# Moving projection tails, maxima transposes and head variances within the attention steps of a four-layer sequence model

## The chip, the cores and the metric

One core of a Trainium2 chip runs the whole program in one launch. The metric is device time in microseconds (us). Everything is fp32.

## The reference

The input is four sequences (batches) of 512 tokens with 288 features. A rotation comes first, then three transformer layers, numbered 0, 1 and 2 here, each with adaptive layer norms, 16-head attention of head size 18, and a feed-forward part; in layer 2 that is a mixture of four experts. The change touches attention alone. In layer 1 every head's q and k are normalised before they are used:

```python
qkv = (xn @ w_qkv + b_qkv).reshape(B, N, 3, H, hd)
q, k, v = (qkv[:, :, 0], qkv[:, :, 1], qkv[:, :, 2])
q = _ln(q, 1e-05, qn_g, qn_b)
k = _ln(k, 1e-05, kn_g, kn_b)
attn = jnp.einsum('bqhd,bkhd->bhqk', q, k) * scale
attn = jax.nn.softmax(attn, axis=-1)
o = jnp.einsum('bhqk,bkhd->bqhd', attn, v).reshape(B, N, C)
```

Layers 0 and 2 compute the same without the two `_ln` lines.

## The kernel before

Layer and batch make one number n = 4·layer + batch, from 0 to 11. `attend` (L1207) runs n's attention in 32 **steps**: four groups of four heads, and eight steps s = 0 to 7 in each. The order of the work on TensorE, VectorE and ScalarE is written out by hand: instructions stay in the order in which the Python code issues them. Only transfers and GpSimd's work are placed by a scheduler.

A step issues the following.

- **Scores for maxima**, `maxima` (L1119): two matmuls into the PSUM tile `p_s`, queries by keys, and on VectorE one reduction of the tile to row maxima, into `M`. They run LOOK = 10 steps ahead, so from step 22 on they belong to the next n.
- **Scores for weights**, `weigh` (L1137): two matmuls into `p_st`, keys by queries, and one exponential on ScalarE. The four score matmuls contract over 32 rows each, so they sit in the four 32-row strips of the array and run side by side. `p_s` and `p_st` share one pool of two PSUM buffers (L82).
- **Transposed maxima**, `take_maxima` (L1129), once in a group at s = 6: four transposes of `M` into `p_m`, and a VectorE subtraction from the queries. The first use of those queries is two steps later.
- **Values**, `give_values` (L1237), in even steps: four matmuls into `p_av`; after a group's last, ScalarE copies the sum to `o`, and five transfers store it.
- **Filling work** (`fill`): generators that are advanced until a budget `left` is spent. It grows in each step by total/32, half a microsecond more in odd steps and half a microsecond less in even ones (L1223). A generator yields the cost of what it issued.

The fill holds above all `project(n+1)` (L1044), which makes the next n's q, k and v. It has five q/k slices (`qk_job`, PSUM tile `p_qk`, 126 rows of output each, the last 72) and four v slices (`v_job`, `p_v`), taken in pairs. Of the 288 features, 256 are contracted in two **dense** matmuls for each slice (128 rows each). The last 32 are its **tail**: one matmul on 32 rows, and the two tails of a pair use different strips. Then each slice is evicted, in layer 1 in two halves:

```python
scalar.activation(sq, p[0:w], AF.Square, bias=bias)
vector.tensor_scalar(t, p[0:w], bias, None, ALU.add)
yield 0.0
matmul(pv[0:w], varsel..., sq, start=True, stop=True)
scalar.activation(rs, pv[0:w], AF.Ln, bias=eps5[0:w])
scalar.activation(rs, rs, AF.Exp, scale=-0.5)
yield 0.86
vector.scalar_tensor_tensor(t, t, gains[0]..., rs, ...)
nc.gpsimd.tensor_scalar(t, t, gains[1]..., None, ALU.add)
```

The second half (the variance matmul `p_var` and what follows) is kept in `later` and issued behind the next pair's dense matmuls. Each slice ends in a transfer from its `stage` tile (three buffers) to a scratch tensor `qd` in HBM (L1076). When all five are on their way, eight transfers read `qd` back in the padded layout of the scores: four for Q, four for K, one for each strip (L1113). K's four need the fifth slice, Q's only the first three. `there` then tells `attend` that the next n may be used.

Behind the projection's first part come `finish` (L1180, the output projection `p_o` of n−1, four pieces), the remaining v slices, and the layer norm transposes `p_t` for n−1's feed-forward part. What is left when the 32 steps end is issued then, and `mlp(n−1)` follows.

Projection tiles, `p_m`, `p_o`, `p_t` and `p_var` share one pool of three PSUM buffers (`pmm`, L79).

Of the kernel before, what the change touches and what calls it, by code (L numbers as in the profile page):

```python
# [9 lines left out]
F32 = mybir.dt.float32  # L10
# [6 lines left out]
B, T, C = 4, 512, 288  # L17
# [4 lines left out]
H, HD, HS = 16, 18, 32  # L22
VS = HD + 1
NG = 4
HP = 7
QP = HP * HD
QK = 2 * C
NQ = -(-QK // QP)
# [19 lines left out]
def cond_seq_kernel(ctx: ExitStack, tc: tile.TileContext, a: dict, out: bass.AP):  # L48
# [18 lines left out]
    dma = nc.sync.dma_start  # L67
# [159 lines left out]
    Q = [t[:, 0:NG * T].rearrange("p (g t) -> p g t", t=T) for t in store]  # L227
    K = [t[:, NG * T:2 * NG * T].rearrange("p (g t) -> p g t", t=T) for t in store]
# [7 lines left out]
    zero_row = rows.tile([4, NG * T], F32, name="zero_row")  # L236
# [398 lines left out]
    NB, LOOK = 3 * B, 10  # L635
# [33 lines left out]
    def layernorm(l, part, b, dst, norm):  # L669

        for _ in norm:
            pass
        for _ in to_featT(dst, b, XN.pop((l, part, b)), modT[l][:, 2 * part + 1], modT[l][:, 2 * part], 2 + part):
            yield 0.6
# [353 lines left out]
    with tc.tile_pool(name="attn", bufs=2) as at:  # L1028
# [14 lines left out]

        def project(n, norm):  # L1044

            l, b = divmod(n, B)
            wqk, wv = WA[l][:2]
            h = hT[0]
            yield from layernorm(l, 0, b, h, norm)
            qd = scratch.tile([2 * H, HD, T], F32, tag="qd", name=f"qd{n}")  # L1050
            flat = qd.rearrange("h d t -> (h d) t")

            def qk_job(m):
                w = min(QP, QK - m * QP)
                cols = slice(m * QP, m * QP + w)
                p = pmm(f"p_qk{n}_{m}")

                def evict():
                    bias = QB[l][0:w, m:m + 1]
                    t = at.tile([QP, T], F32, tag="stage", name=f"stage{n}_{m}", bufs=3)[0:w]  # L1060
                    if l != 1:
                        scalar.activation(t, p[0:w], AF.Identity, bias=bias, scale=scol[0:w, m:m + 1])
                    else:
                        tmp = at.tile([128, 2, T], F32, tag="e", name=f"tmp{n}_{m}", bufs=6)
                        sq, rs = tmp[0:w, 0, :], tmp[0:w, 1, :]
# [3 lines that stand above are left out]
                        pv = pmm(f"p_var{n}_{m}")  # L1069
                        matmul(pv[0:w], varsel.rearrange("p h d -> p (h d)")[0:w, 0:w], sq, start=True, stop=True)  # L1070
# [3 lines that stand above are left out]
                        vector.scalar_tensor_tensor(t, t, gains[0][0:w, m:m + 1], rs, ALU.mult, ALU.mult)  # L1074
                        nc.gpsimd.tensor_scalar(t, t, gains[1][0:w, m:m + 1], None, ALU.add)
                    dma(flat[cols], t)  # L1076
                return p[0:w], 0.86, lambda k, r: (wqk[r, k, cols], h[r, k, :]), evict

            def v_job(j):
                p = pmm(f"p_v{n}_{j}")  # L1080

                def evict():
                    (scalar.copy if j % 2 else vector.tensor_copy)(
                        V[n % 2][:, j, :, 0:HD], p[:, :C].rearrange("p (h d) -> p h d", d=HD))
                    yield from ()
                return p[:, :C], 0.49, lambda k, r: (h[r, k, j * 128:(j + 1) * 128], wv[r, k, :]), evict

            jobs = [(qk_job, m) for m in range(NQ)] + [(v_job, j) for j in range(NT)]
            later = []
            for i in range(0, len(jobs), 2):  # L1090
                pair = []
                for job, arg in jobs[i:i + 2]:
                    p, cost, operands, evict = job(arg)
                    for k in range(KW):
                        matmul(p, *operands(k, slice(0, 128)), start=(k == 0), stop=False)
                        yield cost
                    pair.append((p, operands, evict))
                for e in later:
                    yield from e
                for q, (p, operands, evict) in enumerate(pair):  # L1100
                    matmul(p, *operands(KW, strip(q)), start=False, stop=True)

                later = [e for e in [evict() for p, operands, evict in pair] if next(e, None) is not None]
                yield 0.95
                if i <= NQ - 1 < i + 2:
                    for e in later:
                        yield from e
                    later = []

                    src = qd.rearrange("(s g i) d t -> s i d g t", s=2, i=4)  # L1110
                    for s, t in enumerate((Q[n % 2], K[n % 2])):
                        for q in range(4):
                            dma(t[q * HS:q * HS + HD], src[s, q])  # L1113
                    for q in range(4):
                        dma(Q[n % 2][q * HS + HD:q * HS + VS], zero_row[q:q + 1].rearrange("a (g t) -> a g t", t=T))
                    there.add(n)
                    yield None

        def maxima(G, step):  # L1119
# [9 lines left out]
        def take_maxima(G):  # L1129

            n, g = divmod(G, NG)
            p = pmm(f"p_m{G}")
            for j in range(NT):
                transpose(p[:, j * 128:(j + 1) * 128], M[G % 2][:, j].rearrange("p h r -> p (h r)"), ident)
            vector.tensor_sub(Q[n % 2][:, g, :], Q[n % 2][:, g, :], p)
# [70 lines left out]

        def attend(n, fill, total, norms):  # L1207

            left = 0.0
            for step in range(8 * NG):  # L1210
                g, s = divmod(step, 8)
                G = NG * n + g
                ahead, mstep = divmod(8 * G + s + LOOK, 8)
                if ahead < NG * NB:
                    while ahead // NG not in there:
                        next(fill)
                    maxima(ahead, mstep)
                E.append(weigh(G, s))
                if s == 8 - 2 and G + 1 < NG * NB:
                    take_maxima(G + 1)  # L1220
                if s % 2 == 0:
                    give_values()
                left += total / (8 * NG) + (0.5 if s % 2 else -0.5)  # L1223
                next(norms, None)
                while left > 0:
                    cost = next(fill, "end")
                    if cost == "end":
                        break
                    left -= cost or 0.0
                if s % 2:  # L1230
                    ready.append((G, s // 2))
            for _ in fill:
                pass
            for _ in norms:
                pass

        def give_values():  # L1237

            if not ready:
                return  # L1240
            G, c = ready.pop()
            if c == 0:
                PO[0] = pacc(f"p_av{G}")
            sum_values(G, PO[0], c, E[:2])
            del E[:2]
            if c == NT - 1:
                t = at.tile([128, T], F32, tag="o", name=f"o{G}", bufs=3)
                scalar.copy(t, PO[0])
                n, g = divmod(G, NG)
                if g == 0:  # L1250
                    S[n] = (scratch.tile([H, T], F32, tag="sd", name=f"sd{n}"),
                            scratch.tile([H, HD, T], F32, tag="od", name=f"od{n}"))
                dma(S[n][0][4 * g:4 * g + 4, :], t.rearrange("(h r) c -> h r c", r=HS)[:, HD])
                for h in range(4):
                    dma(S[n][1][4 * g + h], t[h * HS:h * HS + HD])
# [29 lines left out]
        E, ready, PO, S, there, norms = [], [], [None], {}, set(), {}  # L1285
# [22 lines left out]
        new = project(1, norm1)  # L1308
        for _ in range(4):
            next(new)  # L1310
        for t in range(LOOK):
            maxima(*divmod(t, 8))
            if t == 8:
                take_maxima(0)
            next(rest, None)
            next(new)
            if t == 5:
                projection_bias(0)
        for n in range(NB):
            l, b = divmod(n, B)  # L1320
            last = n and divmod(n - 1, B)

            fill, side, total = [], [], 0.0
# [6 lines left out]
            if n + 1 < NB:  # L1330
                if n:
                    new = project(n + 1, norm)
# [26 lines left out]
            if n == NB - 1:  # L1359
                fill = [routed(norms[1], 1), place(0), fill[0]]  # L1360
# [196 lines left out]
```

## Time and profile before

| | us |
|---|---|
| median of three runs | 2061.03 |
| lowest and highest | 2056.3, 2065.32 |
| the profiled execution | 2073.42 |
| its span | 2071.7 |

The profiled execution is 12.4 us above the median. The mean granted TensorE clock over its span is 0.954. The page gives TensorE 1887.7 us of busy time (91% of the span), VectorE 928.4, ScalarE 783.6, GpSimd 251.9. The attention steps lie between about 188 and 1655 us.

In the timeline a step begins where the first weight load of its `p_s` stands. From the first of step 0 to that of step 31, an n takes:

| n | layer of n / of the projection in it | from, us | 31 steps, us |
|---|---|---|---|
| 2 | 0 / 0 | 431.05 | 86.9 |
| 3 | 0 / 1 | 563.50 | 92.5 |
| 4 | 1 / 1 | 695.92 | 92.8 |
| 5 | 1 / 1 | 828.71 | 103.3 |
| 6 | 1 / 1 | 971.94 | 92.5 |
| 7 | 1 / 2 | 1106.31 | 86.8 |
| 8 | 2 / 2 | 1233.02 | 86.7 |

A timeline row gives start, duration, engine, line, operation, output<-inputs, shapes, how many instructions were merged, and in brackets the engine's idle time before it with what ended it. Most rows carry L60, the line of the helper that keeps the order. PEld is a weight load, PE a matmul; each fp32 matmul stands as two of each. "issue" means that no wait shows.

### The profile page before, as it was taken

How to read it: one execution, taken by the hardware profiler on the slowest of the kernel's cores; microseconds unless marked ns; L12 is line 12 of the kernel's file. 1: busy time of each engine (PE TensorE's matmuls, PEld its weight loads, DVE VectorE, ACT ScalarE, POOL GpSimd, SP SyncE). 2: the span in 40 equal slices, each digit the busy share in tenths (PEclk: the TensorE clock that was granted, in tenths of full speed). 3: DMA queues.
4: the chain of work that ended last, by engine and by line, in shares of the span. 5: the costliest groups of instructions: out<-in, count | busy, mean ns of one | idle time of the engine just before them, and what ended most of it. 6: DMA issues, size and time to landing. Idle time of an engine off the chain costs nothing. (4 is left out here: it accounts for less than half of the span.)

```text
span 2071.7 us, 26248 instructions
## 1 busy us (share of the span) xinstructions
PE 1887.7 (91%) x10269; PEld 935.6 (45%) x10269; DVE 928.4 (45%) x1953; ACT 783.6 (38%) x1169; POOL 251.9 (12%) x362
## 2 busy tenths in 40 slices
PE   6769879999999999899999999998987888999998
PEld 4544223343523434234234353333332266788886
DVE  6764646346164362552644626345576234211111
ACT  5122454444254343453544434434444222221221
POOL 1000010001010020010100000000000122233232
PEclk9578999999999999999999999999999689999999
DMA  3212152031131221511213112161212265576673
GB/s 97 71 40 62 36 147 84 22 89 36 25 85 30 70 62 42 136 42 54 72 26 77 42 54 81 21 134 35 83 46 66 86 222 167 182 242 200 211 241 97
DMA packets 89419, 187.23 MB, mean 90 GB/s; under 512 B 25453, under 2 KB 50456, under 8 KB 86802
## 3 DMA queue, kind: packets, MB, share of 16 engines
q1 hardware_dynamic: 77462, 103.39, 19.1%
q0 software_dynamic: 11248, 79.79, 11.9%
q10 hardware_dynamic: 584, 2.36, 0.3%
q8 instruction: 81, 1.33, 0.3%
q14 instruction: 44, 0.36, 0.1%
HBM read 152.49 MB, written 55.45 MB: 100 GB/s over the span
## 5 line engine op out<-in xcount | busy, mean ns | idle before, releaser
L60 ACT ACTIVATE e<-p_st 128x1024 f32<-128x1024 f32 x384 | 392.7, 1023 | 650.7 <-PE p_st L60 646.3
L60 DVE TENSOR_REDUCE store<-p_s 128x2 f32<-128x1024 f32 x384 | 470.3, 1225 | 364.5 <-PE p_st L60 320.7
L60 PE MATMUL p_s<-store 32*128 32x512 f32 x1536 | 442.2, 648 | 82.5 <-DVE store L60 81.3
L60 PE MATMUL p_st<-store 32*128 32x512 f32 x1536 | 445.7, 659 | 0.9 <-DVE store L60 0.9
L60 PEld LDWEIGHTS p_s<-store 32*128 32x128 f32 x1536 | 120.0, 185 | 315.3 <-DVE store L60 228.2
L60 PE MATMUL p_av<-e,store 128*32 128x512 f32 x1536 | 212.8, 627 | 2.2 <-ACT e L60 2.2
L60 PE MATMUL p_he<-hTe,store 128*128 128x256 f32 (+1 forms) x1026 | 188.4, 390 | 4.2 <-DVE hTe L60 4.2
L60 PE MATMUL p_ye<-store,hide 128*128 128x288 f32 x684 | 171.4, 409 | 0.0
L60 PEld LDWEIGHTS p_he<-hTe,store 128*128 128x128 f32 (+1 forms) x1026 | 151.4, 191 | 37.7 <-issue 13.6
L695 POOL TENSOR_TENSOR x<-x,gated 128x288 f32<-128x288 f32 x80 | 63.9, 799 | 841.6 <-DVE gated L60 841.6
L60 PE MATMUL p_qk<-hT,wqk 128*126 128x512 f32 (+1 forms) x360 | 163.1, 622 | 0.3 <-DVE store L60 0.3
L60 ACT ACTIVATE hide<-p_he,store 128x256 f32<-128x256 f32 x171 | 68.5, 478 | 245.1 <-PE p_he L60 244.3
L60 PE MATMUL p_h<-hT,w 128*128 128x512 f32 (+1 forms) x432 | 153.5, 610 | 5.2 <-DVE store L60 5.2
L60 PEld LDWEIGHTS p_ye<-store,hide 128*128 128x128 f32 x684 | 128.2, 190 | 36.7 <-ACT hide L60 2.3
L60 PE MATMUL p_y<-w,hid 128*128 128x288 f32 x576 | 141.8, 407 | 0.0
L60 DVE TENSOR_TENSOR gated<-p_y,gate 128x288 f32<-128x288 f32 x32 | 14.6, 457 | 283.0 <-PE p_y L60 283.0
L60 PEld LDWEIGHTS p_y<-w,hid 128*128 128x128 f32 x576 | 108.8, 190 | 35.5 <-issue 6.1
L60 PEld LDWEIGHTS p_st<-store 32*128 32x128 f32 x1536 | 118.2, 187 | 12.1 <-issue 9.1
L60 PEld LDWEIGHTS p_h<-hT,w 128*128 128x128 f32 (+1 forms) x432 | 62.1, 189 | 95.1 <-issue 84.9
L60 PE MATMUL p_o<-wp,oc 126*128 126x288 f32 (+1 forms) x288 | 99.4, 468 | 1.3 <-DVE oc L60 1.3
L60 PEld LDWEIGHTS p_qk<-hT,wqk 128*126 128x126 f32 (+1 forms) x360 | 47.1, 178 | 95.9 <-issue 94.3
L60 DVE COPY hTe<-p_te 128x512 f32<-128x512 f32 x19 | 13.1, 690 | 169.2 <-PE p_tf L60 117.8
(248 smaller groups left out, 1728.8 us busy)
## 6 DMA issues: line engine op xcount, KB each, us to landing
store<-qd SPq DMA_DIRECT2D x96, 144.0 KB
qd<-stage SPq DMA_DIRECT2D x48, 252.0 KB
od<-o SPq DMA_DIRECT2D x192, 36.0 KB
rd<-rd SPq DMA_DIRECT2D x12, 576.0 KB
oc<-od SPq DMA_DIRECT2D x24, 252.0 KB
rb<-rd SPq DMA_DIRECT2D x24, 252.0 KB
etab<-in_L_cond_w_dram SPq DMA_DIRECT2D x4, 1296.0 KB
etab<-in_L_cond_w_dram SPq DMA_DIRECT2D x8, 576.0 KB
```

Of the source, the lines that this page charges most:

```text
L60: ins = f(*args, **kw)
L695: nc.gpsimd.tensor_add(x[b][:, j, :], x[b][:, j, :], t)
```

## The change

- A pair's tails are issued at the start of a step, right behind that step's scores: the generator yields "strips" ahead of them, which ends a step's filling work, and the next step takes them up.
- `take_maxima` moves from s = 6, right behind the scores, to the end of s = 5, behind the filling work. The budget of that step is smaller by 0.6.
- In layer 1 the last q/k slice's second half is no longer forced out behind its own tail. Like the others, it comes behind the next pair's dense matmuls (two v slices), and the transfers back from `qd` (`send`) come behind it. In layers 0 and 2 `send` stays where the transfers were.
- `stage` gets a fourth buffer, `o` has two instead of three.

```diff
@@ project: evict()
-                    t = at.tile([QP, T], F32, tag="stage", name=f"stage{n}_{m}", bufs=3)[0:w]
+                    t = at.tile([QP, T], F32, tag="stage", name=f"stage{n}_{m}", bufs=4)[0:w]
@@ project
+            def send():
+
+                src = qd.rearrange("(s g i) d t -> s i d g t", s=2, i=4)
+                for s, t in enumerate((Q[n % 2], K[n % 2])):
+                    for q in range(4):
+                        dma(t[q * HS:q * HS + HD], src[s, q])
...
+                there.add(n)
+
...
                 for e in later:
                     yield from e
+                if l == 1 and i <= NQ + 1 < i + 2:
+                    send()
+                    yield None
+                yield "strips"
                 for q, (p, operands, evict) in enumerate(pair):
                     matmul(p, *operands(KW, strip(q)), start=False, stop=True)
 
                 later = [e for e in [evict() for p, operands, evict in pair] if next(e, None) is not None]
                 yield 0.95
-                if i <= NQ - 1 < i + 2:
-                    for e in later:
-                        yield from e
-                    later = []
...
-                    there.add(n)
+                if l != 1 and i <= NQ - 1 < i + 2:
+                    send()
                     yield None
@@ attend
-            left = 0.0
+            left, strips = 0.0, False
...
                 E.append(weigh(G, s))
-                if s == 8 - 2 and G + 1 < NG * NB:
-                    take_maxima(G + 1)
+                if strips:
+                    left -= next(fill)
+                    strips = False
                 if s % 2 == 0:
                     give_values()
-                left += total / (8 * NG) + (0.5 if s % 2 else -0.5)
+                take = s == 7 + 8 - LOOK and G + 1 < NG * NB
+                left += total / (8 * NG) + (0.5 if s % 2 else -0.5) - (0.6 if take else 0.0)
                 next(norms, None)
                 while left > 0:
                     cost = next(fill, "end")
-                    if cost == "end":
+                    strips = cost == "strips"
+                    if cost == "end" or strips:
                         break
                     left -= cost or 0.0
+                if take:
+                    take_maxima(G + 1)
@@ give_values
-                t = at.tile([128, T], F32, tag="o", name=f"o{G}", bufs=3)
+                t = at.tile([128, T], F32, tag="o", name=f"o{G}", bufs=2)
```

The order of the built programs on TensorE, behind the scores of each step, for one n with a layer 1 projection (n = 4). "dense qk" is one dense matmul, "tails" the pair's two, "m" the four transposes of the maxima, "o" one piece of the output projection:

| step | before | after |
|---|---|---|
| 9 | variance ×2 | dense qk, variance |
| 13 | dense v ×2 | dense qk, m |
| 14 | m, values, variance | values, dense v |
| 15 | variance, tails | dense v, variance |
| 16 | values | values, variance |
| 17 | variance (the fifth slice's), o | nothing |
| 18 | values | tails, values, dense v ×2 |
| 19 | o | dense v ×2, variance (the fifth slice's) |
| 20 | values, o | values |
| 21 | o | o, m |
| 22 | m, values | values |
| 23 | dense v ×2 | o ×2 |

On VectorE, the multiplication that ends the fifth slice's normalisation (`stage<-stage,qn_g,tmp`, 72 rows) stands right behind the reduction of step 17 before, and right behind that of step 21 after. It is so in n = 3, 4, 5 and 6. On GpSimd and in the transfer queue, the addition, the transfer to `qd` and K's four transfers follow it in both, with nothing new between. The scores for maxima of step 22 are the first to read the next n's K; their two matmuls read strips 0 and 1.

More of the change, by code (lines that the diff above doesn't have):

```diff
@@ L1086, in v_job @@
                 return p[:, :C], 0.49, lambda k, r: (h[r, k, j * 128:(j + 1) * 128], wv[r, k, :]), evict
+            def send():
[3 more added lines that the diff above has]
+                        dma(t[q * HS:q * HS + HD], src[s, q])
+                for q in range(4):
+                    dma(Q[n % 2][q * HS + HD:q * HS + VS], zero_row[q:q + 1].rearrange("a (g t) -> a g t", t=T))
+                there.add(n)
             jobs = [(qk_job, m) for m in range(NQ)] + [(v_job, j) for j in range(NT)]
@@ L1104, in project @@
                 yield 0.95
-                if i <= NQ - 1 < i + 2:
-                    for e in later:
-                        yield from e
-                    later = []
[L1110 to L1115, printed above, removed]
-                    there.add(n)
+                if l != 1 and i <= NQ - 1 < i + 2:
+                    send()
                     yield None
@@ L1315, in cond_seq_kernel @@
             next(rest, None)
-            next(new)
+            if next(new) == "strips":
+                next(new)
             if t == 5:
```

## The prediction

> **What bounds the kernel now.** I read the page's busy times first (TensorE 91% of the span), then the timeline step by step, since a share says nothing about which wait ends last. Two neighbouring steps of n = 1:
>
> ```profile
> 331.89 0.70 PE L60 MATMUL p_s<-store 32*128 32x512 f32 x2
> ...
> 332.96 1.07 PE L60 MATMUL p_av<-e,store 128*32 128x512 f32 x8
> 333.06 1.23 DVE L60 TENSOR_REDUCE store<-p_s 128x2 f32<-128x1024 f32 x1 [1.42 <-PE p_st L60]
> ...
> 334.35 0.70 PE L60 MATMUL p_s<-store 32*128 32x512 f32 x2 [0.32 <-DVE store L60]
> ...
> 336.27 0.20 PEld L60 LDWEIGHTS p_qk<-hT,wqk 128*72 128x72 f32 x2 [0.76 <-issue]
> ...
> 337.28 0.19 PEld L60 LDWEIGHTS p_s<-store 32*128 32x128 f32 x2 [0.80 <-DVE store L60]
> ```
>
> The first step has only values behind its scores: 1.07 us of scores, 1.0 of values, then TensorE waits until the reduction frees the PSUM buffer, 1.17 + 1.23 + 0.06 = **2.46 us** from scores to scores. This is a step's floor. The second has tails and one dense matmul: 334.35 to 336.27 is 1.92 = 1.07 + 0.85, so tails right behind scores cost their 0.85 alone; the dense one takes until 337.28, 1.01. So a step takes the larger of 2.46 and its TensorE work. The work, read the same way from block starts: scores 1.07, values 1.0, a dense q/k matmul 0.85, a pair of q/k tails 0.85, a dense v 0.48, a piece of `p_o` 1.84, transposes `p_m` 0.6 alone and 0.4 behind dense work; and 0.2 for each change between scores or tails, full-height matmuls and values (0.1 of weight load that nothing hides, 0.1 of drain).
>
> I priced every step of a few n by this rule and held it against the measured 31 steps of the front's table: n = 2 gives 85.9 (measured 86.9), n = 3, 4, 6 give 89.1 (92.5 to 92.8), n = 5 gives 89.1 (103.3). The rests have names. Layer 0/2 projections: 1.0 where `p_t` waits for its input in the last steps. Layer 1: 1.07 where two variances stand in step 9, 1.7 to 2.0 in step 16, where the reduction stands behind two multiplications that wait for ScalarE, 0.8 to 0.9 for `p_t`. In n = 5, weights are loaded at the same time, and VectorE stands behind a late transfer and then a missing `stage` buffer:
>
> ```profile
> 865.73 0.69 DVE L60 TENSOR_TENSOR oc<-oc,rb 126x512 f32<-126x512 f32 x1 [2.31 <-DMA rb<-rd]
> 868.91 0.75 DVE L60 TENSOR_SCALAR stage<-p_qk,qkb 126x512 f32<-126x512 f32 x1 [1.17 <-POOL stage L1075]
> ```
>
> Last, the fifth slice's way to the scores in n = 4, from the timeline around 751 us:
>
> ```profile
> 751.49 0.75 DVE L60 SCALAR_TENSOR_TENSOR stage<-stage,qn_g,tmp 72x512 f32<-72x512 f32 x1 [1.16 <-ACT tmp L60]
> 752.39 1.56 POOL L1075 TENSOR_SCALAR stage<-stage,qn_b 72x512 f32<-72x512 f32 x1 [4.81 <-issue]
> 753.98 0.29 SPq L1076 DMA_DIRECT2D qd<-stage  x1
> 756.40 1.39 SPq L1113 DMA_DIRECT2D store<-qd  x4
> 763.86 0.70 PE L60 MATMUL p_s<-store 32*128 32x512 f32 x2
> ```
>
> From the multiplication to the issue of K's transfers are 4.91 us. The windows view shows them moving data from 757.3 to 762.1 (130 to 157 GB/s, then nothing): 4.8 for four strips, 1.2 each. Step 22 starts at 763.86, 1.7 after the last byte. No wait shows, because the multiplication stands five steps ahead.
>
> **The change, part by part.**
>
> *Tails behind the scores.* Counted over the built programs (the expert tiles left out), changes of array mode fall from 943 to 903: 40 × 0.2 = 8 us of TensorE work. Here the Trainium skill would have me book them: "TensorEngine Tiling (Array Packing)", section Key Properties, says that changing the tiling mode drains TensorE. The row says that a drain costs 0.2, but in a step under the floor it costs nothing. And tails that wait for the next scores end a step's fill early: in n = 4, steps 17 and 27 are left empty (1.07 of work, 2.46 of time) while step 18 has tails, values and two dense v, 4.1. So the pricing by steps decides, not the 8 us.
>
> *Maxima.* Before, `p_m` lay under step 6's reduction, and the step took 2.65, 0.2 over the floor. Now it ends step 5; its last transpose needs that step's reduction, so the scores can start no earlier than 2.46 + 0.3 (one transpose with its drain) = 2.76. Up to 0.3 instead of 0.2, four times in an n: +0.4 where step 5 is short, less where fill hides it.
>
> *Fill spread anew.* The last `p_t` come behind step 31's scores, where `mlp` waits for the PSUM buffer until 2.46 anyway; they fill 1.1 of 1.4 idle us. The 1.0 in the late steps goes.
>
> Sums by the rule for 31 steps: layer 0/2 projections 87.0 (86.9, 86.8, 86.7 now): +0.1 to +0.3 each. Layer 1 projections 92.4, with the three small waits gone (the variances now stand singly, each with a reduction between): against 92.5 that is nothing. n = 0 +0.7, n = 9 +0.4, n = 10 and 11 together −1.4. All but layer 1: about **+0.5**.
>
> *Buffers.* The fourth `stage` buffer takes away the 1.17 wait and what hangs on it in n = 5; the wait for `rb` stays, some 1.2 us of it on TensorE. `o` with two: each is stored within 12 us of its copy (the slowest, 853.6 to 865.4), and the next use of the buffer is 16 steps, 45 us, away. Nothing.
>
> *The last variance a pair later.* This one decides. The multiplication now stands behind the reduction of step 21, one step before the scores that need it. Count from that step's scores: reduction at 1.19, multiplication 1.14 behind it at 2.33, K's transfers issued 4.91 later at 7.24, first byte 0.9 later, two strips 2.4, and 0.5 until the arrival is seen (the write to `qd` shows this: its data end about 755.9, the next issue comes at 756.40): **11.0**. TensorE is ready at about 4.3 (scores 1.07, a piece of `p_o` 1.84, then `p_m`: two v slices hold two of the three PSUM buffers until step 28, so it waits for the eviction of `p_o`). So TensorE idles 6.7 us, with everything else queued behind that `p_s`: weights scores, values, and ScalarE and VectorE with them. The rule gave step 21 3.49; it becomes 11.0: **+7.5**. Bounds: +6.5 if the write takes 2.0 rather than 2.4 (621.20 to 623.21 in n = 3) and the strips come as reckoned, +9.6 if the four strips arrive together. The same PSUM shortage makes the second `p_o` in step 23 wait for its forerunner: +0.6.
>
> *The clock behind it.* After the 3.75 us of idle TensorE in n = 5 the granted clock is half:
>
> ```profile
> 863.00:870.00 7.00, 4.10 (x22) 0.82 (x20) 3.52 (x6) 2.45 (x4) 1.56 (x1) 1.00 0.50 157
> 870.00:877.00 7.00, 6.15 (x21) 2.25 (x21) 3.21 (x4) 1.02 (x1) 0.00 (x0) 0.52 0.23 64
> ```
>
> The seventh column is the clock, 0.52. Steps 13 and 14 took 4.24 and 4.92 for 2.46 and 3.76: +2.9. The skill, "TensorE: Matmul & The Clock Gate", section What's actually happening, has the rule: after an idle window of about 3.4 us half rate, and full rate after a busy one of the same length. That makes 3.4 us of work take twice its time, +1.7. An idle 6.7 us is sure to hold most of two such windows, so every one of the four stalls should lead to it. I take **+2.7**, near the row.
>
> A layer 1 projection: 92.4 + 7.5 + 0.6 + 2.7 = 103.2. Against 92.5, 92.8, 92.5: +10.7, +10.4, +10.7. n = 5: 103.2 + 1.2 for `rb`, against 103.3: +1.1. Sum **+32.9**, with the rest **+33.4**. The profiled execution would go from 2073.4 to 2106.8; in proportion (1.6%) the median from 2061 to **2094**.
>
> **The rivals.**
>
> 1. *K comes in time.* If the first two strips are there when TensorE asks, a layer 1 projection takes 92.4 or a little more, and n = 5 falls by about 9: 2061 − 8 = 2053. For it: all that the other parts say. Against it: the 4.91 us between multiplication and issue are measured, and nothing shortens them. It needs K landed within 4.3 us of step 21's scores, before the transfers are even issued (7.24). 7%.
> 2. *Half the stall.* Strips land sooner, the clock stays up (idle below 3.4 us): +3 or 4 in each of three n, n = 5 falls by 5: 2061 + 5, no change to tell. 10%.
> 3. *The clock stays low for longer.* Between 1614 and 1648 it stays at half for 34 us although TensorE is busy. If each stall drags its whole rest of an n with it, +5 more each: 2114. Against it: n = 5 recovers within 7 us, twice. 12%.
>
> My forecast has 71%. Its own bounds: with +6.5 and +1.7 for stall and clock, 2061 + 25; with +9.6 and +4.5, 2061 + 50; step pricing is good to about 1 us in an n. The range 2072 to 2114 holds that and the top of rival 2. A difference of under 0.5% (10 us) can't be told from none here. Faster by more 7%, within 10%, slower 83%.
>
> **What would show it.** In the timeline of n = 3 to 6, step 22's `p_s` with 6 to 7 us of idle time ended by `store<-qd`, and half clock behind it; steps 9 and 16 without their waits; no wait for `stage` in n = 5; steps 5 of a group at 2.76 where short. The forecast is wrong if that `p_s` starts within 5 us of step 21's, or if n = 3, 4, 6 come out under 95 us for 31 steps.

## The result, and the profile after

The changed kernel takes 2131.4 us in the median of its four runs (2121.38 to 2137.31), the kernel before 2063.18: the ratio is **1.030**, 95% interval 1.026 to 1.035. Measured once more later, in six runs beside 29 of the kernel before, the ratio was 1.024 (1.020 to 1.028). The direction was as forecast, the size was not: the forecast was 2094, and its range ended at 2114. The profiled execution took 2121.38 us with a granted clock of 0.946, against 2073.42 and 0.954.

Part 1 of the page after, busy time by engine:

```profile
span 2119.7 us, 26236 instructions
...
PE 1901.9 (90%) x10269; PEld 938.8 (44%) x10269; DVE 930.7 (44%) x1953; ACT 784.2 (37%) x1169; POOL 254.2 (12%) x362
```

VectorE, ScalarE and GpSimd do what they did. TensorE's busy time grew by 14.2 us with the same number of matmuls, so some of them ran at a lower clock; the rest of the 48 us in the spans is waiting.

Steps found as before, this is how much later each n begins in the changed kernel's profile, and what its 31 steps take:

| n | begins later by, us | 31 steps before | after |
|---|---|---|---|
| 0 | 1.5 | 84.5 | 81.6 |
| 1 | 1.1 | 90.7 | **99.3** |
| 2 | 9.7 | 86.9 | 87.6 |
| 3 | 12.6 | 92.5 | **103.0** |
| 4 | 23.2 | 92.8 | **103.0** |
| 5 | 33.5 | 103.3 | 106.9 |
| 6 | 37.1 | 92.5 | **103.2** |
| 7 | 48.3 | 86.8 | 87.6 |
| 8 | 49.1 | 86.7 | 87.6 |
| 9 | 50.0 | 87.4 | 90.9 |
| 10 | 53.5 | 97.7 | 101.9 |
| 11 | 57.9 | 97.3 | 89.6 |

The row of n = 11 counts 30 steps, to the first weight load of step 30's `p_st`, as its last ten steps issue no `p_s`; to step 31 it is 101.0 before and 91.6 after. Between n = 9 and n = 11 the difference goes with the clock: it was at half for 0, 6.8 and 41.0 us of the 31 steps before, and for 6.8, 13.7 and 22.6 us after. So the changed kernel, 57.9 us behind where n = 11 begins, shows only 48 at the end.

Four other places stand out. In n = 3, 4 and 6 the stall is where it was forecast. The timeline of the changed kernel from step 21 of n = 3:

```profile
637.55 0.70 PE L60 MATMUL p_s<-store 32*128 32x512 f32 x2 [0.32 <-DVE store L60]
...
639.86 0.74 DVE L60 SCALAR_TENSOR_TENSOR stage<-stage,qn_g,tmp 72x512 f32<-72x512 f32 x1
...
640.76 1.56 POOL L1076 TENSOR_SCALAR stage<-stage,qn_b 72x512 f32<-72x512 f32 x1 [10.58 <-issue]
...
642.35 0.29 SPq L1077 DMA_DIRECT2D qd<-stage  x1
644.39 1.39 SPq L1094 DMA_DIRECT2D store<-qd  x4
...
647.72 2.40 PE L60 MATMUL p_s<-store 32*128 32x512 f32 x3 [5.98 <-DMA store<-qd]
...
651.01 1.23 DVE L60 TENSOR_REDUCE store<-p_s 128x2 f32<-128x1024 f32 x1 [8.54 <-PE p_st L60]
...
652.81 1.22 PE L60 MATMUL p_s<-store 32*128 32x512 f32 x2
```

TensorE has nothing to do for 5.98 us, ended by K's transfer; VectorE, which needs the scores, waits 8.54. From scores to scores step 21 takes 10.14 us (9.84 and 10.03 in n = 4 and 6). Behind it a pair of score matmuls shows 1.22 us where step 21's shows 0.70: half clock, from 643.7 to 653.9 us.

The fourth place, n = 1, was not forecast. One step there, step 7, takes 10.44 us instead of 3.04. The changed kernel's timeline:

```profile
325.32 0.55 DVE L60 RECIPROCAL sums<-sums 128x64 f32<-128x64 f32 x1 [5.13 <-DMA sums<-sd]
...
327.60 2.07 PE L60 MATMUL p_st<-store 32*128 32x512 f32 x4 [3.60 <-DVE store L60]
```

The reciprocal of n = 0's sums waits 5.13 us for its transfer, and the reductions that free the PSUM buffers stand behind it. In the kernel before it found its data there without a wait:

```profile
320.10 0.54 DVE L60 RECIPROCAL sums<-sums 128x64 f32<-128x64 f32 x1
```

Why the transfer is late shows in the transfer queue's own timeline (with ScalarE's copy to `o` between its rows), first of the changed kernel, then of the kernel before:

```profile
301.04 0.29 SPq L326 DMA_DIRECT2D mrow<-gr  x1
...
304.78 0.59 ACT L60 COPY o<-p_av 128x512 f32<-128x512 f32 x1 [0.83 <-PE p_av L60]
304.81 5.17 SPq L143 DMA_DIRECT2D wqk<-in_L_cond_w_qkv_dram  x4
...
320.16 0.51 SPq L1263 DMA_DIRECT2D sd<-o  x1
...
323.49 0.35 SPq L1166 DMA_DIRECT2D sums<-sd  x1
```

```profile
288.42 0.29 SPq L326 DMA_DIRECT2D mrow<-gr  x1
...
292.32 5.28 SPq L143 DMA_DIRECT2D wqk<-in_L_cond_w_qkv_dram  x4
...
306.73 0.51 SPq L1253 DMA_DIRECT2D sd<-o  x1
...
310.33 0.34 SPq L1161 DMA_DIRECT2D sums<-sd  x1
```

`mrow<-gr` is the end of the modulations, the last of n = 0's filling work. The first of the next weights reuse the modulations' buffers, and the loads keep the order of the program, so all are issued behind it, some 18 us of issuing one after another, and the store of the sums (`sd`) stands behind the loads. All of it slid by 12.5 to 13.4 us. On VectorE the reciprocal stands right behind the reduction of step 5 in both; the reductions of steps 6 and 7 wait with it, so the lost time shows in step 7.

### The profile page after: what moved, and what is told of

Read it like the earlier page. It is cut to its first block, busy times and chain, and to the rows that moved or that the text cites. A ratio compares the mean times of both kernels' runs of the same rounds, so it can differ in the third digit from the quotient of the medians.

```text
span 2119.7 us, 26236 instructions
## 1 busy us (share of the span) xinstructions
PE 1901.9 (90%) x10269; PEld 938.8 (44%) x10269; DVE 930.7 (44%) x1953; ACT 784.2 (37%) x1169; POOL 254.2 (12%) x362
## 5 line engine op out<-in xcount | busy, mean ns | idle before, releaser
L60 PE MATMUL p_s<-store 32*128 32x512 f32 x1536 | 454.0, 661 | 108.2 <-DVE store L60 83.4
L60 PE MATMUL p_st<-store 32*128 32x512 f32 x1536 | 452.3, 666 | 3.6 <-DVE store L60 3.6
L60 PE MATMUL p_qk<-hT,wqk 128*126 128x512 f32 (+1 forms) x360 | 170.4, 639 | 0.3 <-DVE store L60 0.3
L60 PEld LDWEIGHTS p_st<-store 32*128 32x128 f32 x1536 | 118.9, 189 | 10.7 <-issue 6.1
L60 PEld LDWEIGHTS p_av<-e,store 128*32 128x32 f32 x1536 | 30.9, 110 | 151.6 <-issue 149.7
L60 PE MATMUL p_o<-wp,oc 126*128 126x288 f32 (+1 forms) x288 | 94.0, 447 | 3.0 <-DVE gated L60 2.2
```

The costliest lines, as they stand in the source:

```text
L60: ins = f(*args, **kw)
```

## The experiments

Each kernel below was profiled and timed beside the kernel before. "31 steps" are read from its profile.

**The last variance undone** (`late_undone`), in the changed kernel:

```diff
                 for e in later:
                     yield from e
-                if l == 1 and i <= NQ + 1 < i + 2:
-                    send()
-                    yield None
                 yield "strips"
...
-                if l != 1 and i <= NQ - 1 < i + 2:
+                if i <= NQ - 1 < i + 2:
+                    for e in later:
+                        yield from e
+                    later = []
                     send()
                     yield None
```

> The changed kernel with one part undone: in layer 1 the last variance and the eight transfers back from qd are issued right behind their own pair's tails, as before. Everything else is as in the changed kernel. By the built order the fifth slice's multiplication then stands behind the reduction of step 19, two steps earlier. Stall theory (K lands 11.0 us after the scores of the step whose reduction the multiplication follows): steps 19 to 21 hold about 9.7 us of work, so 1.3 us of stall are left instead of 6.7, and TensorE's clock hardly drops. n = 3, 4, 6 take 93.5 to 96 us for 31 steps instead of 103.0, n = 5 about 97 instead of 106.9: in all some 35 us less than the changed kernel, about 2095 us. Rival (the slowdown is spread over empty steps and a lower clock everywhere): less than 15 us off, above 2116. Either way n = 1 keeps its 10.4 us step 7.

Measured: ratio to the kernel before 1.006 (1.003 to 1.009), 2082.98 us. n = 3, 4, 6 take 95.5, 95.2, 93.6 us and n = 5 100.2; n = 1 keeps 98.6. So the delay of this one variance makes up most of the loss: against the changed kernel n = 3 to 6 give back 7.5, 7.9, 6.6 and 9.5, together 31.5 us. n = 5 was expected at 97, and the clock to hold: 3.4 us at half clock remain in step 22 of n = 3, 4 and 5. The step 22 wait of n = 3 in this kernel's timeline:

```profile
631.94 0.74 DVE L60 SCALAR_TENSOR_TENSOR stage<-stage,qn_g,tmp 72x512 f32<-72x512 f32 x1
...
636.48 1.39 SPq L1094 DMA_DIRECT2D store<-qd  x4
...
639.86 2.27 PE L60 MATMUL p_s<-store 32*128 32x512 f32 x3 [0.61 <-DMA store<-qd]
```

0.61 us of wait are left of 5.98. Step 19's scores began at 629.63, step 22's at 639.83: 10.2 us, as from step 21's in the changed kernel (10.14). Between multiplication and issue lie 4.54 us here and 4.53 there.

**The same part alone, in the kernel before** (`late_alone`). The edit is the `send` part of the change, with the tails left where they were:

```diff
                 for e in later:
                     yield from e
+                if l == 1 and i <= NQ + 1 < i + 2:
+                    send()
+                    yield None
...
-                if i <= NQ - 1 < i + 2:
-                    for e in later:
-                        yield from e
-                    later = []
...
+                if l != 1 and i <= NQ - 1 < i + 2:
+                    send()
                     yield None
```

> The kernel before with one part of the change alone: in layer 1 the last variance and the transfers back come behind the next pair's dense matmuls. Here the multiplication stands behind the reduction of step 19, not of step 21. Stall theory by the same 11.0 us: steps 19 to 21 hold 8.3 us, so step 22 waits 2.7 us in n = 3, 4 and 6, perhaps with one stretch of half clock (1.7) behind it: 95 to 98 us instead of 92.5. In n = 5 the same or hidden behind its other waits. In all +9 to +16, about 2075 us. Rival (what costs is that the variance is late at all, wherever it lands): about +33 as in the changed kernel, 2095 us.

Measured: 1.012 (1.009 to 1.016); 97.9, 100.3 and 99.7 us in n = 3, 4, 6, n = 5 unchanged at 103.4. That is +5.4 to +7.5 in each, where +2.5 to +5.5 was expected. The median, 2097.3 us, lies near the rival's 2095, but by another way: it is 29 above the kernel before, and these three n hold 20 of it. The row of step 22 in n = 3:

```profile
625.46 0.75 DVE L60 SCALAR_TENSOR_TENSOR stage<-stage,qn_g,tmp 72x512 f32<-72x512 f32 x1 [1.16 <-ACT tmp L60]
...
629.96 1.39 SPq L1092 DMA_DIRECT2D store<-qd  x4
...
632.83 1.82 PE L60 MATMUL p_s<-store 32*128 32x512 f32 x3 [0.73 <-DMA store<-qd]
```

K is late by 0.73 us only. The rest is step 19, where the piece of `p_o` waits for ScalarE behind the variance (4.77 instead of 2.92), a waiting step 21 (3.69), and step 22 (6.03 instead of 2.65), where the strips' wait, transposes, values and a piece of `p_o` now meet; in n = 3 at full clock, in n = 4 and 6 with 3.4 and 6.8 us of half clock (7.40 and 8.80). Neither theory's account came out; the 11 us from step 19's scores to step 22's did (10.9, 11.4 and 11.3).

**TensorE kept busy through the stall** (`kept_busy`), in the changed kernel. These matmuls compute nothing that is used:

```diff
             p = pbig(f"p_s{G}_{step}")
+            if g == 0 and step == 0 and n // B == 1 and n > 0:
+                for _ in range(6):
+                    matmul(p[:, 0, :], ident, hT[1][:, 0, :], start=True, stop=True)
```

> The changed kernel with six more 128 x 128 by 128 x 512 matmuls ahead of step 22's scores for maxima in n = 3 to 6, which write the PSUM tile that the scores then overwrite: TensorE works through most of the stall, nothing else changes. If the slow steps behind the stall are the clock's doing, the stall itself stays (step 21 about 10 us), no half clock follows, steps 22 and 23 go back from 5.1 and 6.1 us to about 2.7 and 4.5, and four n gain about 4 us each: 12 to 17 us off, about 2117 us. If they are slow because queued work is caught up, nothing changes.

Measured: 1.017 (1.011 to 1.022), 2104.52 us. The same stretch behind the stall of n = 3, in the windows view of the changed kernel and of this one (the seventh column is the clock):

```profile
640.00:660.00 20.00, 12.93 (x54) 4.67 (x57) 5.73 (x10) 2.09 (x3) 3.74 (x4) 0.74 0.16 37
```

```profile
640.00:660.00 20.00, 17.37 (x79) 6.58 (x77) 7.22 (x12) 3.61 (x4) 3.90 (x4) 1.00 0.14 37
```

Step 21 still takes 10.24 us (9.94 and 10.12 in n = 4 and 6), as K is as late as ever, but the clock stays at 1.00. Step 22 falls from 5.12 to 3.32, step 23 from 5.92 to 5.48: the clock cost **2.2 us** in n = 3. In n = 4 one stretch of half clock, 3.4 us, stays. The 31 steps of n = 3 to 6 fall by 2.1, 1.0, 3.3 and 2.1. That adds up to 8.5 us, less than the 12 to 17 expected; n = 9 to 11 were 12.4 us shorter too, with 15.9 us at half clock there instead of 43.1.

**A larger budget for n = 0** (`n0_budget`), in the changed kernel:

```diff
-                total += 7.2
+                total += 9.6
```

> The changed kernel with one number changed: the fill budget of n = 0 is 9.6 instead of 7.2 for the modulations, so that their last matmuls come in step 26 instead of behind step 31. Queue theory for n = 1: the modulations' end releases the weight loads, which stand in the transfer queue ahead of the store of n = 0's sums; with the modulations earlier the queue is empty sooner, the reciprocal in step 7 of n = 1 no longer waits, step 7 takes about 3 us instead of 10.4, and 31 steps of n = 1 take 90 to 92 us instead of 99.3. About 9 us less than the changed kernel, 2122 us; the layer 1 stalls stay as they are. Rival (the wait is of another cause, say the two buffers of o or the order of the transfers): n = 1 stays at 99 us.

Measured: 1.016 (1.011 to 1.022), 2107.54 us. n = 1 falls from 99.3 to 89.6 us and its step 7 to 2.98: the queue theory holds, and the rivals of another cause fall. (The time stands beside 2117.19, the median of the changed kernel when it was measured again.) But part of the wait turned up elsewhere: n = 0's last step takes 7.50 us instead of 4.99. From its timeline:

```profile
304.77 1.35 DVE L189 TENSOR_REDUCE wmean<-wqk 128x64 f32<-128x1152 f32 x1 [5.01 <-DMA wqk<-in_L_cond_w_qkv_dram]
...
307.31 1.22 PE L60 MATMUL p_s<-store 32*128 32x512 f32 x2 [6.36 <-DVE store L60]
```

A reduction on the new weights now stands in front of the one that the scores need, and waits for the same loads. From the changed kernel's profile, n = 2 begins only 3.9 us earlier.

**The maxima alone, with and without the smaller budget** (`maxima_moved`, `maxima_no_cut`), in the kernel before; the second leaves out the last term:

```diff
-                if s == 8 - 2 and G + 1 < NG * NB:
-                    take_maxima(G + 1)
...
-                left += total / (8 * NG) + (0.5 if s % 2 else -0.5)
+                take = s == 7 + 8 - LOOK and G + 1 < NG * NB
+                left += total / (8 * NG) + (0.5 if s % 2 else -0.5) - (0.6 if take else 0.0)
...
+                if take:
+                    take_maxima(G + 1)
```

> The kernel before with the maxima's transposes at the end of step 5 of a group and that step's budget smaller by 0.6, as in the change; nothing else. By the built order the smaller budgets add up: the fifth slice's multiplication comes behind the reduction of step 19 instead of 17, and n = 0's modulations end behind step 31. Knock-on theory: n = 1 gets its wait in the reciprocal (+8), n = 3, 4, 6 a short stall in step 22 (+1 to +3 each, as with the last variance undone), in all +12 to +20, about 2083 us. Rival (only the place of the transposes counts): +0.1 to +0.3 in a group's step 5, 48 groups at most, so under 5 us in all, 2068 us.

> As the kernel with the maxima moved alone, but the step's budget isn't made smaller. By the built order the multiplication stands behind the reduction of step 17 and the modulations end in step 27, both as before. Knock-on theory: n = 1 and n = 3 to 6 as before, within 1 us each, the whole within 5 us of the kernel before, 2066 us; the difference to the kernel with the cut, some 15 us, is what the 0.6 costs. Rival (place of the transposes): both kernels the same.

Measured: 1.013 (1.005 to 1.020) with the cut and 1.003 (0.999 to 1.006) without it. The two intervals just touch, but the profiles tell the kernels apart: n = 1 and n = 3 to 6 take some 3 to 7 us more with the cut. Four times 0.6 us of bookkeeping in an n cost more than the move itself. Without it n = 1 and n = 6 stayed within 2.2 us and n = 3 and 4 grew by 3.9, not by under 1: steps 17 and 18 take 5.34 and 3.69 us in n = 3, with the clock at half for 6.8 us from 617.7 on. With the cut n = 1 grew by 4.7 us and n = 0's last step by 2.5; n = 3, 4, 6 by 7.1 to 7.5, more than expected. The stall of step 22 is there (6.80 us for 2.65 in n = 3), but as much is lost in a step that nobody had in view, step 12, at 7.66 us for 3.23 in each of the three, with half clock from near its end. In n = 3:

```profile
608.05 0.75 DVE L60 TENSOR_SCALAR stage<-p_qk,qkb 126x512 f32<-126x512 f32 x1 [3.36 <-DMA qd<-stage]
```

VectorE waits for one of the three `stage` buffers to be written out. The spread of the fill that comes with the cut needs the fourth one, in every layer 1 projection of this kernel. In the changed kernel, which has it, step 12 of n = 3 takes 3.92.

**The tails alone** (`tails_alone`), in the kernel before: the `yield "strips"` ahead of the tails and what takes it up in `attend`.

> The kernel before with the pairs' tails right behind the next scores, and nothing else. The multiplication stands behind the reduction of step 17 as before, the modulations end in step 27 as before. Step theory (steps under the floor of 2.46 us gain nothing from fewer changes of array mode): layer 1 and layer 0/2 projections within 1 us of before, the whole within 5 us, 2066 us. Rival by the count of mode changes: about 8 us less, 2058 us.

Measured: 1.008 (1.005 to 1.011), slower, so both expectations were wrong. No stall came: the 31 steps grew by 2.6 to 2.8 us in n = 0, 2, 7, 8 and by 1.9 in n = 3, 4, 6. The steps show how: in n = 3 step 5 went from 2.98 to 2.45 and step 6 from 2.67 to 4.76. Work left a step that had to last 2.46 us anyway and made the next one, with values and transposes, the longer. In the full change the transposes fill the emptied step 5.

**The buffers alone** (`buffers_alone`): `stage` with four buffers, `o` with two, in the kernel before.

> The kernel before with four stage buffers and two of o, and nothing else; the order of the instructions is the same. Only n = 5 waited for stage (1.17 us, then half clock): it goes from 103.3 us for 31 steps to 98 to 102; all else the same. 2 to 5 us less than before, which the times can't tell from nothing. Rival (two buffers of o make ScalarE wait): n = 1 or n = 5, where transfers are slow, get longer.

Measured: 0.999 (0.995 to 1.003). The 1.17 us wait for `stage` in n = 5 is gone, and n = 5 still takes 103.4: `rb` landed later in this execution.

```profile
867.67 0.69 DVE L60 TENSOR_TENSOR oc<-oc,rb 126x512 f32<-126x512 f32 x1 [3.96 <-DMA rb<-rd]
```

**The changed kernel again** (`after_again`).

> The changed kernel once more, in five rounds, to see what of it varies. In the first comparison the times grew by 62 to 68 us, the two profiled executions only by 48. Theory (what varies is the half clock in sparse stretches: whether a 3.4 us stretch comes out busy enough depends on where it begins): the stalls of n = 3, 4, 6 are the same within 0.5 us (103.0 to 103.2 for 31 steps), n = 1 and n = 5 within 1 us, and the difference between executions sits in n = 9 to 11 (before 282.4, after 282.3 in the first pair; 270 to 296 possible) and goes with the granted clock, about 2 us for each 0.001 of it. Rival: the layer 1 stalls themselves vary by several us.

Measured: 1.024 (1.020 to 1.028), median 2117.19 us. n = 3, 4, 6 take 103.1, 103.3 and 103.1, n = 1 99.5, n = 5 106.9: the stalls did not vary between the two. n = 9 to 11 took 274.1 us where the first execution took 282.3. Over all 10 runs of this kernel the time runs from 2107.6 at a mean clock of 0.955 to 2137.3 at 0.938, some 1.7 us for each 0.001; over 73 runs of the kernel before from 2055.7 at 0.963 to 2084.8 at 0.947, some 1.8.

**Mended** (`mended`, `mended_more`): the variance as in `late_undone`, n = 0's 9.6, and for layer 1 projections 5.5 (or 6.5) in place of 4.5 in the budget.

> The changed kernel with three things mended: the last variance and the transfers back right behind their own tails, the budget of n = 0 at 9.6, and that of a layer 1 projection larger by 1.0 (5.5 for 4.5). The multiplication then stands behind the reduction of step 18, and steps 18 to 21 hold some 13 us, more than the 10.2 to 10.9 that K needs: no stall in step 22, n = 3, 4, 6 at 91 to 94 us for 31 steps, n = 5 at 96 to 99. With n = 1 at 89.6 and the last step of n = 0 still long (7.5), the sum is within 10 us of the kernel before: 2060 to 2076 us. If a stall in step 22 stays, the 10.2 us are wrong.

> As the mended kernel, with the layer 1 budget larger by 2.0 (6.5). The multiplication stands behind the reduction of step 17, where it was in the kernel before. By the stall theory nothing is left to gain over the mended kernel in step 22: n = 3, 4, 6 within 1.5 us of it. If they fall by more, K was still late there.

Measured: 1.001 (0.998 to 1.003) and 1.006 (1.003 to 1.009). With 5.5 n = 3, 4, 6 take 93.2 us each and n = 5 93.5, 9.8 less than before; n = 1, which begins 7.5 us later, and n = 2 take most of that back. No wait for K is left: from its timeline,

```profile
630.32 0.74 DVE L60 SCALAR_TENSOR_TENSOR stage<-stage,qn_g,tmp 72x512 f32<-72x512 f32 x1
...
634.84 1.39 SPq L1094 DMA_DIRECT2D store<-qd  x4
...
640.79 0.19 PEld L60 LDWEIGHTS p_s<-store 32*128 32x128 f32 x2 [0.17 <-PE p_m L60]
```

the scores of step 22 come 5.95 us behind the issue and wait for TensorE itself; in the stalls they came 3.3 behind it. With 6.5, n = 3, 4, 6 took 95.6, 95.6 and 97.3: no gain from an earlier K, as expected, but 2.4 to 4.1 us more, not within 1.5: step 17 is crowded (variance and `p_o`, 5.57 us, 7.23 in n = 6). With 5.5, n = 5 came out below the 96 to 99 expected.

**The kernel before with n = 0's budget at 9.6 and the buffers** (`before_budget`).

> The kernel before with the four stage buffers (and two of o) and n = 0's budget at 9.6 for 7.2: the modulations end in step 23 of n = 0 instead of 27, so the weights' loads are issued some 10 us earlier. Queue theory: the slow steps 27 and 28 of n = 0 and 0 and 1 of n = 1 (4.98, 3.42, 4.92 and 4.36 us) fall to about 2.5 to 3 us each, 4 to 6 us in all; n = 5 as in the kernel with the buffers alone. 2058 to 2066 us, at the edge of what can be told. Rival: the modulations' own weights come no earlier and the steps wait for them instead, nothing gained.

Measured: 1.001 (0.999 to 1.003), nothing gained. n = 0's last step grew to 6.99 us, the same wait for the new weights as in `n0_budget`, and n = 1 gave back 1.4. Here `rb` was waited for 1.57 us only and n = 5 took 94.2, which the times don't show. No version beat the kernel before.

## Why the prediction fell short

*What bounds the kernel, and the rule of 2.46 us.* It held. Steps with little work still take 2.45 to 2.46 in the changed kernel, and the three small waits of layer 1 did go: step 9 of n = 4 takes 2.99 for 4.03, step 16 3.12 for 4.49.

*The last variance a pair later.* Right in mechanism; in size nearly, and there with some luck. Forecast were +10.7, +10.4 and +10.7 for n = 3, 4, 6; +10.6, +10.2 and +10.6 came. Two terms were each a little large: the way from step 21's scores to step 22's takes 9.8 to 10.1 us, not 11.0 (4.53 us from multiplication to issue for 4.91, and 3.3 from there to the scores for 3.8), and the clock costs 2.2, not 2.7, as the run that kept TensorE busy shows. The pricing of the other steps was about 1 us short. These errors, −0.9, −0.5 and about +1.2, cancel. The row behind the 2.7 was misread: step 14, put at 3.76, takes 4.10 in n = 3 and 6 of the kernel before at full clock, so steps 13 and 14 of n = 5 show 2.6 more, not 2.9. The second `p_o`'s 0.6 is there: it waits 0.55 us for the first one's eviction.

*All but layer 1: "about +0.5".* **This is the step that failed.** Where n = 11 begins, the profiles are 57.9 us apart; the 31 steps of n = 3 to 6 hold 34.9 of it, with 32.9 forecast, so 23 (1.5 of it ahead of n = 0) lie where the forecast had about 2. The largest term is n = 1. n = 0 was priced by its own steps, +0.7 for the smaller budgets. What it issues last was not followed into the transfer queue. Its modulations ended 12.6 us later, the weights' loads behind them, and the sums behind those: +8.6 in n = 1, with 13.7 us at half clock instead of 3.4. The order of instructions on TensorE showed the modulations slide from step 27 to step 31; the prediction counted their matmuls and not whom their end releases. The larger budget for n = 0 shows the cause by taking the wait out of n = 1. The Trainium skill, "DMA: Bandwidth & Descriptors", section "Anatomy of one DMA — SWDGE (gpsimd) path", says that DMA engines do not wait on semaphores, any such wait is held by the issuing sequencer. These transfers are SyncE's, and the rows agree as far as the order goes: `o` was copied at 304.78 and its `sd` store issued at 320.16, with only the loads in between. n = 2, 7 and 8 were 0.7 to 0.9 longer against 0.1 to 0.3, the last step of n = 0 2.5 and that of n = 2, with `mlp`, 2.2. Why the last two grew is not shown. n = 9 and 10 lost 3.5 and 4.1 with 6.8 us more of half clock in each, for which the forecast had no term outside the stalls.

*Buffers.* The `stage` wait went, as forecast. The wait for `rb`, taken as 1.2 us on TensorE, was the larger term: VectorE waits 3.06 in the changed kernel, steps 12 and 13 take 6.21 and 4.16, and n = 5 grew by 3.6, not 1.1. The wait was 3.03 in the other profile of this kernel; over all the kernels it runs from 1.09 to 5.57, and why `rb` lands when it does stays open.

```profile
899.41 0.69 DVE L60 TENSOR_TENSOR oc<-oc,rb 126x512 f32<-126x512 f32 x1 [3.06 <-DMA rb<-rd]
```

"Nothing" was right for the two buffers of `o`, but the fourth `stage` buffer was underrated: without it the maxima's new spread alone loses a step of 7.66 us in n = 3, 4 and 6. The whole change with three buffers was not run.

*Tails and maxima.* Right not to book 8 us for fewer mode changes. The maxima's step 5 takes 2.72 (forecast 2.76). Of the 0.6 that is taken from the budget the prediction priced what it does within n = 0, not how far it shifts everything behind it: alone it separates 1.013 from 1.003.

*The rivals.* K in time (1) and half the stall (2) are out: the wait is 5.98 us. Of a clock that stays low for longer (3), half is true: 10.2 us of half clock go with each stall, three stretches and not one. But the first 3.3 to 4.0 us of it lie in the stall itself, and the rest cost 2.2 in n = 3, not 5 more. (What was held against it was misread: the second half clock of n = 5 before lasted 10.2 us, from 887.0 to 897.3, not 7.)

*From profile to time.* Scaling the profile's difference to the median was the last step, and it added an error of its own: the profiles differ by 48 us in span, the first runs by 68, the later ones by 50. Both kernels scatter over some 30 us with the granted clock, so four runs settle the difference to about 10 us only. The profile of the kernel before had drawn a slow n = 11, 101.0 us with 41 at half clock; with the same order of instructions the kernel with the buffers alone took 87.8 there. So of the 37 us between 2094 and 2131 some 23 lie in the steps ahead of n = 11, n = 1 first, and the rest in which executions were compared. The 2117 of the repeat is still above the range.

## What to carry to other kernels

When filling work is moved, follow the last thing it releases, through the transfer queue, to the first instruction that cannot move; a small cut in a budget shifted an end by four steps here (the modulations', from step 27 to behind step 31). A result that goes through HBM and back needs its whole way priced (here some 10 us from the step's scores), and room for it in steps ahead of its reader. Steps that only just fill their minimum are no free ground: emptying one and filling the next lengthens the sum.

## What was not expected of the hardware

The clock drops without an idle stretch. In n = 9 of the changed kernel no long wait occurs, yet (windows view, the seventh column is the clock):

```profile
1425.40:1432.20 6.80, 5.17 (x34) 1.75 (x38) 5.12 (x8) 3.58 (x5) 0.00 (x0) 1.00 0.68 91
1432.20:1439.10 6.90, 6.90 (x26) 1.47 (x18) 1.73 (x4) 3.06 (x4) 0.00 (x0) 0.51 0.45 158
```

Just ahead of the second row stands a step with scores alone; step 8, behind it, took 7.23 us for 3.71. The clock's record changes in stretches of 3.41 us. Counted between 188 and 1690 us over ten profiles (the two kernels and the first eight experiments), with TensorE's matmuls and weight loads taken together: of the stretches at full clock that were less than 45% busy, all 51 were followed by half clock; of those 45 to 60% busy, 41 of 72; above 60%, 45 of 4034 (some matmul records are missing; why these 45 turned is not shown). So in these profiles about half busy is where it turns, and a step of scores alone, 1.07 us of 2.46, lies below that. The Trainium skill, "TensorE: Matmul & The Clock Gate", section "What's actually happening", has half rate follow an idle window, and windows that run freely, whatever the kernel does. The second would fit a clock that differs from run to run of the same program, which no run here tests; the first is too mild for this case: the stretch from 1428.8 to 1432.2 was 52% busy, with no gap over 1.31 us.
